# Routed experts of two batches: 46 tiles of their own against 40 shared tiles

## The chip, the core and the metric

The kernel runs on one NeuronCore of a Trainium2 chip. Five engines work side by side, each through its own queue in program order: PE (TensorE, matrix products and transposes), DVE (VectorE), ACT (ScalarE), POOL (GpSimd, here also the indirect DMAs) and SP (SyncE, here only DMA issues). A wait in a queue holds everything behind it. The metric is device microseconds of one execution. Before the change three runs gave 2401.68 us as median (2397.92 to 2402.32).

## What is computed

Two batches of 2048 tokens, 256 channels. First a bidirectional Mamba layer whose result is added to x with a gate; then a layer norm with scale and shift per batch, and a mixture of experts:

```
scores = softmax(xt @ gate_w.T);  top_vals, idx = top_k(scores, 2)
xs = xt[:, None, :] * weights[:, :, None]
y += sum_k( (silu(xs @ w1[e].T + b1[e]) @ w2[e].T + b2[e]) * (xs @ w3[e].T + b3[e]) )   # k with idx == e
z  = silu(xt @ sw1.T) * (xt @ sw2.T) @ sw3.T
out = x + gb * (y + z)
```

There are 8 experts, and each token goes to 2 of them. `gb` is a gate for each channel and batch.

## The kernel before, in words

The program has a long Mamba stage and then the expert stage (lines 928 to 1358), which is all that the change touches but for a few small DMAs. The expert stage has three parts.

**Units with fronts beside them** (lines 1278 to 1326). A batch has 4 chunks of 512 tokens. The shared expert of a chunk is 4 `hidden` units (line 1124: 16 matmuls in the trace, two PSUM banks, then silu on ACT and a product on DVE, line 1137) and 2 `result` units (line 1140: 16 matmuls, then an addition on DVE, line 1149). The list of units `interleaved` (line 1289) holds 37 places, k = 0 to 36, for the four chunks of the first batch and the first two of the second. What DVE and ACT do for a unit is put into their queues only after the next unit's matmuls (`unit`, line 1267). The table `beside` (line 1298) is an order written out by hand: it says which step of which chunk's `front` (line 988) is put in ahead of unit k. The steps are LOAD (two DMAs), OPEN (gate and add the Mamba result, then statistics, DVE), NORM (4 activations, ACT), MODULATE (scale and shift, DVE), TURN (8 transposes on PE, 2 copies on ACT), CHOOSE (router logits on PE, maximum and difference on DVE, exp on ACT) and RANK (two best experts, 14 small DVE operations). Seven PSUM banks, taken in turn (`bank`, line 935), serve units, TURN, CHOOSE and routing alike: an operation on PE waits until the bank used seven takes earlier has been read.

**Routing.** `route` (line 1057) works in two steps. The first counts on DVE; the second takes three small matmuls (lines 1073 to 1075) and then some 15 DVE operations, which give each token its two row numbers (`slots`) and each tile its expert (`owners`). `scatter` (line 1101) then writes 32 blocks of 128 weighted rows to DRAM (`xs`): a copy on ACT and an indirect DMA on POOL each. For the first batch that is routed at k = 15 and 16 and scattered two blocks a unit from k = 17.

**Tiles** (`expert_tiles`, line 1195). An expert's tokens are padded to tiles of 256 rows. Each batch has 23 tiles (`NTS`, the worst case), 46 in all. `load_tile` (line 1155) brings, three tiles ahead, three weight matrices of 256 KB, the biases and the tile's rows `xg`, all on SP's queue into four buffers. A tile on PE is four transposes of the rows (`qgT`), three products (`qh`, `q3`, `q2`) and four transposes back (`qyT`). ACT makes silu and the second factor with the gate folded in (line 1214, whose bias comes from a small DVE product, line 1206); DVE multiplies (line 1222) and copies `gT` (line 1186); ACT stores the result to `ys`. The second batch's last front steps, its routing and its scatter (4 blocks a tile) lie beside the first 16 tiles (`beside_tile`, `sides`, line 1330). After tile 25 the first batch is gathered chunk by chunk, every fifth tile, by 8 indirect DMAs (`gather`, line 1228); three tiles after a gather `combine` adds both parts to the sum (two DVE additions of 128x1024, line 1250), and SP stores it.

After the last tile the second batch is gathered, beside the shared units of its last two chunks; then come its combinations and stores (lines 1347 to 1358).

```
i = nc.gpsimd.indirect_dma_start(out=xs_d[b][:, :], in_=v, in_offset=None, ...)
tc.declare_no_dep(i, group=f"scatter{b}", reason="each writes rows of its own")
```

Every access is ordered after earlier ones to the same memory unless a line like this one excludes it; a scatter names the whole of `xs` as what it writes.

Of the kernel before, what the change touches and what calls it, by code (L numbers as in the profile page):

```python
# [35 lines left out]
NTS = (2 * T + E * (TS - 1)) // TS  # L36
# [4 lines left out]
def kernel(  # L41
# [26 lines left out]

    xs_d = [dram.tile([NTS * TS, C], F32, tag=f"xs{b}", name=f"xs{b}") for b in range(NB)]
    ys_d = [dram.tile([NTS * TS, C], F32, tag=f"ys{b}", name=f"ys{b}") for b in range(NB)]  # L70
# [63 lines left out]
    with tc.tile_pool(name="mw", bufs=1) as mw, tc.tile_pool(name="mw2", bufs=2) as mw2, \  # L134
# [690 lines left out]
        def early_small():  # L825
            early["wg"] = keep.tile([P, KC, E], F32, tag="wg", name="wg")
            nc.sync.dma_start(out=early["wg"], in_=gate.rearrange("(k p) e -> p k e", p=P))
            for b in range(NB):
                early["gbT", b] = keep.tile([P, KC], F32, tag=f"gbT{b}", name=f"gbT{b}")
                nc.sync.dma_start(out=early["gbT", b],  # L830
                                  in_=mod_d[b][0, 3 * C:4 * C].rearrange("(k p) -> p k", p=P))
# [19 lines left out]
        for s in range(NST + 4 + SPC):  # L851
# [42 lines left out]
            if i < NCH + 1:  # L894
                visit(i, k)
                if s == 8:
                    silu_gate(0)
                if k == 8 and 2 <= i < 2 + NB:
                    nc.sync.dma_start(out=xs_d[i - 2].rearrange("(p n) (m f) -> p (n m) f", p=P, f=P),
                                      in_=bc(ident, NTS * TS // P * 2))  # L900
# [14 lines left out]
        for _ in range(2):  # L915
            open_front(1)

# [10 lines left out]
    with tc.tile_pool(name="fw", bufs=1) as fw, tc.tile_pool(name="f1", bufs=1) as f1, \  # L928
# [27 lines left out]
        wg, gbTs = early["wg"], [early["gbT", b] for b in range(NB)]  # L956
# [19 lines left out]
        tiles = fw.tile([1, NTS, E], F32, tag="tiles", name="tiles")  # L976
        iotas = []
        for v, pattern in ((filled, [[0, E], [TS, NK]]), (tiles, [[1, NTS], [0, E]])):
            n = v.shape[1] * v.shape[2]
            w = f1.tile([v.shape[0], n], I32, tag=f"iota{n}", name=f"iota{n}")  # L980
            nc.gpsimd.iota(w, pattern=pattern, base=0, channel_multiplier=0)
            iotas.append((v, w))
# [72 lines left out]
        slots, owners = {}, {}  # L1055

        def route(b):
# [19 lines left out]
            nt = f1.tile([P, E], F32, tag="nt", name=f"nt{b}")  # L1077
            end = f1.tile([P, E], F32, tag="end", name=f"end{b}")
            nc.vector.tensor_tensor(more, pt.unsqueeze(2).to_broadcast([P, E, NK]), filled, ALU.is_gt)
            nc.vector.tensor_reduce(nt, more, AX.X, ALU.add)  # L1080
            nc.vector.tensor_tensor_scan(end, ones[:, 0:E], nt, 0.0, ALU.mult, ALU.add)
            nc.vector.tensor_tensor(nt, end, nt, ALU.subtract)
            nc.vector.tensor_scalar(nt, nt, float(TS), None, ALU.mult)
            nc.vector.tensor_tensor(past, ps.rearrange("p (e j) -> p e j", e=E),
                                    nt.unsqueeze(2).to_broadcast([P, E, NJ]), ALU.add)
            posf = f1.tile([P, 2, NJ], F32, tag="posf", name=f"posf{b}")
            for n in range(2):
# [4 lines left out]
            after = f1.tile([1, NTS, E], F32, tag="after", name=f"after{b}")  # L1092
            own = f1.tile([1, NTS], F32, tag="own", name=f"own{b}")
            nc.vector.tensor_tensor(after, tiles, end[0:1, :].unsqueeze(1).to_broadcast([1, NTS, E]),
                                    ALU.is_ge)
            nc.vector.tensor_reduce(own, after, AX.X, ALU.add)
            nc.vector.tensor_scalar(own, own, float(E - 1), None, ALU.min)
            owners[b] = fw.tile([1, NTS], I32, tag=f"own{b}", name=f"owner{b}")
            nc.vector.tensor_copy(owners[b], own)

        def scatter(b):
            sc = picks[b][1]
            for j in range(NJ):
                for n in range(2):
# [6 lines left out]
                        out=xs_d[b][:, :], in_=v, in_offset=None,  # L1111
                        out_offset=bass.IndirectOffsetOnAxis(ap=slots[b][:, n, j:j + 1], axis=0))
                    i = getattr(i, "ins", i)

                    tc.declare_no_dep(i, group=f"scatter{b}", reason="each writes rows of its own")
                    tc.add_to_no_dep_group(f"scatter{b}", i)
# [38 lines left out]
        def load_tile(b, i):  # L1155

            e = nc.sync.value_load(owners[b][0:1, i:i + 1], min_val=0, max_val=E - 1)
            ws = f4.tile([P, 3, KC, H], F32, tag="we", bufs=4, name=f"we{b}_{i}")
            xg = f4.tile([P, 2, C], F32, tag="xg", bufs=4, name=f"xg{b}_{i}")
            for n, src in enumerate((w1, w3, w2)):  # L1160
                nc.sync.dma_start(out=ws[:, n, :, :], in_=src[bass.ds(e, 1), :, :]
                                  .rearrange("o (k p) h -> p (o k) h", p=P))
            bs = f4.tile([P, 3, KH], F32, tag="bs", bufs=4, name=f"bs{b}_{i}")
            nc.sync.dma_start(out=bs, in_=b123[:, :, bass.ds(e, 1), :].rearrange("p n o k -> p n (o k)"))
            nc.sync.dma_start(out=xg, in_=tiled(xs_d[b][i * TS:(i + 1) * TS, :]))
            loaded[b, i] = ws, bs, xg
# [16 lines left out]
        def turned_in(b, i):  # L1183
            ps = turn_tile(loaded[b, i][2], f"qgT{b}_{i}")
            gT = f2.tile([P, KC, TS], F32, tag="gT", name=f"gT{b}_{i}")
            nc.vector.tensor_copy(gT, ps)  # L1186
            return gT

        def turned_out(b, i, x3):
            ps = turn_tile(x3, f"qyT{b}_{i}")  # L1190
            yo = f2.tile([P, 2, C], F32, tag="yo", name=f"yo{b}_{i}")
            nc.scalar.copy(yo, ps)
            nc.scalar.dma_start(out=tiled(ys_d[b][i * TS:(i + 1) * TS, :]), in_=yo)

        def expert_tiles(seq, sides):


            for k in range(3):
                load_tile(*seq[k])
            gT, x3 = turned_in(*seq[0]), None  # L1200
            for k, (b, i) in enumerate(seq):
                if k + 3 < len(seq):
                    load_tile(*seq[k + 3])
                ws, bs, _ = loaded.pop((b, i))
                b3 = f2.tile([P, KH], F32, tag="b3", name=f"b3{b}_{i}")
                nc.vector.tensor_tensor(b3, bs[:, 2, :], gbTs[b], ALU.mult)
                hT = f2.tile([P, KH, TS], F32, tag="hT", name=f"hT{b}_{i}")
                y3 = f2.tile([P, KC, TS], F32, tag="x3", name=f"x3{b}_{i}")
                ps = lin(ws, 0, gT, f"qh{b}_{i}")
                for m in range(KH):  # L1210
                    nc.scalar.activation(hT[:, m, :], ps[:, m, :], AF.Silu, bias=bs[:, 0, m:m + 1])
                ps = lin(ws, 1, gT, f"q3{b}_{i}")
                for m in range(KC):
                    nc.scalar.activation(y3[:, m, :], ps[:, m, :], AF.Identity,
                                         scale=gbTs[b][:, m:m + 1], bias=b3[:, m:m + 1])
                if k + 1 < len(seq):
                    gT = turned_in(*seq[k + 1])
                if x3 is not None:
                    turned_out(*seq[k - 1], x3)
                ps = lin(ws, 2, hT, f"q2{b}_{i}")  # L1220
# [4 lines left out]
                sides(k)  # L1225
            turned_out(*seq[-1], x3)

        def gather(b, q):
# [4 lines left out]
            for n in range(2):  # L1233
# [5 lines left out]
                for j in range(JC):  # L1239
                    nc.gpsimd.indirect_dma_start(  # L1240
                        out=v[:, j, :], out_offset=None, in_=ys_d[b][:, :],
# [5 lines left out]
        def combine(b, q, two):  # L1247
            x1 = x1s[b, q]
            for v in two:
                nc.vector.tensor_tensor(x1, x1, v, ALU.add)  # L1250
# [38 lines left out]
        def interleaved(keys):  # L1289

            units, due = [], []
            for k in keys:
# [5 lines left out]
        beside = {1: ((0, 0, CHOOSE), (0, 1, TURN)), 2: ((0, 2, OPEN),),  # L1298
                  4: ((0, 2, NORM), (1, 0, LOAD), (0, 0, RANK)),
                  5: ((0, 1, CHOOSE), (0, 2, MODULATE)), 6: ((1, 1, LOAD), (0, 3, OPEN)), 7: ((0, 2, TURN),),  # L1300
                  8: ((0, 3, NORM), (0, 1, RANK)), 9: ((0, 2, CHOOSE), (0, 3, MODULATE)), 11: ((0, 3, TURN),),
                  12: ((0, 2, RANK),), 13: ((0, 3, CHOOSE),), 14: ((0, 3, RANK),), 17: ((1, 0, OPEN),),
                  18: ((1, 2, LOAD),), 19: ((1, 0, NORM),), 20: ((1, 0, MODULATE), (1, 3, LOAD)),
                  21: ((1, 0, TURN), (1, 1, OPEN)), 22: ((1, 0, CHOOSE),), 23: ((1, 1, NORM),),
                  24: ((1, 1, MODULATE), (1, 0, RANK)), 26: ((1, 1, TURN),), 27: ((1, 1, CHOOSE),),
                  29: ((1, 1, RANK),), 30: ((1, 2, OPEN),), 32: ((1, 2, NORM),), 33: ((1, 3, OPEN),),
                  35: ((1, 3, NORM),)}
        beside_tile = {0: ((1, 2, MODULATE),), 1: ((1, 2, TURN), (1, 3, MODULATE)), 2: ((1, 2, CHOOSE),),
                       3: ((1, 2, RANK), (1, 3, TURN)), 4: ((1, 3, CHOOSE),), 5: ((1, 3, RANK),)}
        scatters, routes = [scatter(0), scatter(1)], [route(0), route(1)]  # L1310
        for k, f in enumerate(interleaved([(0, 0), (0, 1), (0, 2), (0, 3), (1, 0), (1, 1)])):
# [5 lines left out]
            if k in (15, 16):  # L1317
                follow(routes[0])
            unit(f)
            if k > 16:  # L1320
# [9 lines left out]
        def sides(k):  # L1330
            for p in beside_tile.get(k, ()):
                part(*p)
            if k in (6, 7):
                follow(routes[1])
            if k > 7:
                for _ in range(4):
                    follow(scatters[1])
            for q in range(NTC):
                if k == NTS + 2 + 5 * q:
                    twos[q] = gather(0, q)  # L1340
                if k == NTS + 5 + 5 * q:
# [3 lines left out]
        expert_tiles([(b, i) for b in range(NB) for i in range(NTS)], sides)  # L1345
# [69 lines left out]
```

## Time and profile before

The profiled execution took 2401.81 us; the profiler's span is 2400.0 us, so 1.8 us lie around it. Its own time is 0.13 us over the median of the three runs.

| what | value |
|---|---|
| PE busy | 1970.6 us, 82% |
| DVE busy | 2021.3 us, 84% |
| ACT busy | 1619.2 us, 67% |
| POOL busy | 1859.5 us, 77% |
| units with fronts | 1912 to 2059 us |
| tiles | 2059 to 2345 us |
| last shared units, gathers, stores | 2345 to 2400 us |

The shares are means over stages with different limits; the three last rows are read from the timeline. A line of the timeline gives start and duration in us, engine, source line, what is written from what, a count, and in brackets how long the engine sat idle before it and what ended that. A line of a window table gives for each engine busy us (and instructions), then the clock granted to PE (1.00 is full), the busy share of the DMA engines and GB/s.

### The profile page before, as it was taken

The numbers are of one execution on the slowest core, as the hardware profiler recorded it, in microseconds if no ns is written. First come the engines' busy times: TensorE is split into PE (matmuls) and PEld (weight loads), VectorE is DVE, ScalarE is ACT, GpSimd is POOL, SyncE is SP. The second block draws the span as 40 slices with busy tenths as digits, with TensorE's granted clock in tenths as the row PEclk, the third lists the DMA queues.
The fourth block names the chain that finished last, engine by engine and source line by source line (L and its number), as shares of the span: only waits on it lengthen the run. The fifth ranks groups of instructions, "written<-read, shape, count | busy, mean of one in ns | idle before, by whom it ended". The sixth has DMA issues, their size and how long they took to land. (4 is left out here: it accounts for less than half of the span.)

```text
span 2400.0 us, 30317 instructions
## 1 busy us (share of the span) xinstructions
PE 1970.6 (82%) x9512; PEld 1361.7 (57%) x9512; DVE 2021.3 (84%) x2691; ACT 1619.2 (67%) x3375; POOL 1859.5 (77%) x979
## 2 busy tenths in 40 slices
PE   5466878787978888787979788887976699999997
PEld 2133645555646555554656555554555566888884
DVE  5499999989999999999999999999999977542333
ACT  5557787868778787878787777878775334454331
POOL 0367898989999999999999999999999615041305
PEclk9677888898999889888989899998887899999999
DMA  4344447574544544445444444444456231587873
GB/s 161 110 161 155 150 158 226 182 235 165 170 159 158 177 157 169 161 157 176 153 165 163 163 151 167 157 160 159 132 172 224 90 112 73 174 262 239 264 238 114
DMA packets 239974, 403.08 MB, mean 168 GB/s; under 512 B 38818, under 2 KB 171938, under 8 KB 239812
## 3 DMA queue, kind: packets, MB, share of 16 engines
q1 hardware_dynamic: 220724, 370.72, 47.4%
q0 software_dynamic: 6144, 16.79, 2.0%
q10 hardware_dynamic: 12944, 13.64, 1.6%
q8 instruction: 75, 1.23, 0.2%
q14 instruction: 87, 0.71, 0.1%
HBM read 346.54 MB, written 54.53 MB: 167 GB/s over the span
## 5 line engine op out<-in xcount | busy, mean ns | idle before, releaser
L452 POOL TENSOR_TENSOR db<-du,B 128x1024 f32<-128x1024 f32 x452 | 1064.2, 2380 | 14.9 <-DMA B<-bcs 14.9
L496 POOL TENSOR_TENSOR db<-h,C 128x1024 f32<-128x1024 f32 x252 | 599.7, 2381 | 65.7 <-issue 53.9
L471 ACT ACTIVATE da<-dt,w_a 128x512 f32<-128x512 f32 x904 | 594.7, 688 | 79.2 <-DVE dt L336 46.2
L518 PE MATMUL y<-ident,db 128*128 128x128 f32 x4096 | 568.5, 287 | 39.1 <-POOL db L496 36.7
L518 PEld LDWEIGHTS y<-ident,db 128*128 128x128 f32 x4096 | 505.3, 150 | 160.6 <-issue 101.9
L485 DVE TENSOR_TENSOR_SCAN da<-da,hl,db 128x512 f32<-128x512 f32 x460 | 562.9, 1269 | 4.9 <-POOL db L452 3.7
L485 DVE TENSOR_TENSOR_SCAN h<-da,hl,db 128x512 f32<-128x512 f32 x444 | 540.1, 1263 | 15.5 <-ACT da L471 15.5
L491 DVE TENSOR_TENSOR db<-da,C 128x512 f32<-128x512 f32 x460 | 292.2, 676 | 19.8 <-DMA C<-bcs 12.5
L272 PE MATMUL psc<-xp,w_conv 128*128 128x512 f32 x512 | 235.2, 603 | 10.2 <-ACT xp L261 6.4
L255 PE MATMUL psx<-xT,w_in 128*128 128x512 f32 x256 | 155.8, 728 | 102.7 <-ACT hl L506 88.8
L390 PE MATMUL psz<-w_in,xT 128*128 128x512 f32 x256 | 151.1, 723 | 57.0 <-ACT bT L353 32.7
L1110 POOL DMA_INDIRECT xs<-xs,slot x64 | 63.6, 993 | 166.7 <-ACT xs L1106 100.6
L1240 POOL DMA_INDIRECT two<-ys,slot x64 | 63.5, 992 | 159.6 <-DMA ys<-yo 64.3
L342 POOL TENSOR_TENSOR du<-dt,xc 128x512 f32<-128x512 f32 x64 | 81.9, 1281 | 98.5 <-DVE dt L336 98.4
L272 PEld LDWEIGHTS psc<-xp,w_conv 128*128 128x128 f32 x512 | 93.9, 193 | 107.7 <-issue 96.0
L289 PE MATMUL psd<-xc,w_x 128*48 128x512 f32 x128 | 97.4, 932 | 67.7 <-ACT hl L506 47.6
L255 PEld LDWEIGHTS psx<-xT,w_in 128*128 128x128 f32 x256 | 49.8, 223 | 157.2 <-ACT hl L506 110.8
L418 PE MATMUL pso<-w_out,yg 128*128 128x256 f32 x512 | 118.4, 385 | 21.3 <-ACT e L312 20.0
L1186 DVE COPY gT<-qgT 128x512 f32<-128x512 f32 x46 | 31.8, 690 | 108.9 <-PE qgT L939 108.9
L506 ACT COPY hl<-da 128x1 f32<-128x1 f32 x460 | 61.5, 157 | 85.4 <-DVE db L491 82.8
L418 PEld LDWEIGHTS pso<-w_out,yg 128*128 128x128 f32 x512 | 95.6, 192 | 36.5 <-ACT e L312 22.9
L390 PEld LDWEIGHTS psz<-w_in,xT 128*128 128x128 f32 x256 | 53.1, 229 | 109.3 <-issue 42.0
(218 smaller groups left out, 3199.3 us busy)
## 6 DMA issues: line engine op xcount, KB each, us to landing
C<-bcs SPq DMA_DIRECT2D x256, 512.0 KB, 4.4
B<-bcs SPq DMA_DIRECT2D x226, 512.0 KB, 4.3
we<-in_w_dram SPq DMA_DIRECT2D x138, 256.0 KB, 3.7
acc<-acc SPq DMA_DIRECT2D x32, 512.0 KB, 5.5
xs<-ident SPq DMA_DIRECT2D x2, 5888.0 KB, 23.6
xg<-xs SPq DMA_DIRECT2D x46, 256.0 KB, 3.9
ys<-yo ACTq DMA_DIRECT2D x46, 256.0 KB, 3.0
xn<-xn SPq DMA_DIRECT2D x16, 512.0 KB, 5.9
```

The source lines that it names most:

```text
L255: nc.tensor.matmul(ps, w["in"][:, k, d * P:(d + 1) * P], v["xT"][:, k, :], start=(k == 0), stop=(k == KC - 1))
L272: nc.tensor.matmul(ps, w["conv"][:, d, k, :], v["xp"][:, d, k:k + TC], start=(k == 0), stop=(k == 3))
L289: nc.tensor.matmul(ps[:RK + 2 * NS, :], w["x"][:, d, :], v["xc"][:, d, :], start=(d == 0), stop=(d == ND - 1))
L342: nc.gpsimd.tensor_tensor(v["du"][:, d, :], v["dt"][:, d, :], v["xc"][:, d, :], ALU.mult)
L390: nc.tensor.matmul(ps, v["xT"][:, k, j * P:(j + 1) * P], w["in"][:, k, DI:2 * DI], start=(k == 0), stop=(k == KC - 1))
L418: nc.tensor.matmul(ps[:, n, :], v["yg"][:, d, n * P:(n + 1) * P], wo[:, d, :], start=(d == 0), stop=(d == ND - 1))
L452: nc.gpsimd.tensor_tensor(db, bc(ready[i]["du"][:, d, :], NG), live["B", s // 2], ALU.mult)
L471: nc.scalar.activation(da[n], ready[i]["dt"][:, d, :], AF.Exp, scale=w["a"][:, d, m:m + 1])
L485: nc.vector.tensor_tensor_scan(h[n], da[n], x[n], hl[:, d, m:m + 1], ALU.mult, ALU.add)
L491: nc.vector.tensor_tensor(live["db", s][:, n, :], h, live["C", s // 2][:, n, :], ALU.mult)
L496: nc.gpsimd.tensor_tensor(live["db", s], live.pop(("h", s)), live["C", s // 2], ALU.mult)
L518: nc.tensor.matmul(ys["y"][j // 2][:, j % 2, d % 2 * P:(d % 2 + 1) * P], src[:, j * P:(j + 1) * P], ident, is_transpose=True, start=(first ...
```

## The change

All tiles come from one list of 40 (`NT`). A batch-0 expert's whole tiles come first, then one tile for each of the 8 experts that holds its remaining tokens of the first batch and as many of the second as fit, then the second batch's further tiles. At least 9 tiles (`NF`) hold first-batch tokens only; the first batch lies within the first 24 (`N0`). `xs` and `ys` become one tensor each. Because a tile can hold both batches, the gate leaves the tile and goes to `combine`. All fronts and both routings are put among the units, with a new table `beside`; the second scatter runs beside tiles 0 to 7, and the first batch's gathers come every third tile.

```diff
-NTS = (2 * T + E * (TS - 1)) // TS
+NT = 2 * NB * T // TS + E
+NF = -((E * (TS - 1) - 2 * T) // TS)
+N0 = 2 * T // TS + E
+NQ = 3 * E + 1
...
-        tiles = fw.tile([1, NTS, E], F32, tag="tiles", name="tiles")
+        tiles = fw.tile([1, NT, NQ], F32, tag="tiles", name="tiles")
...
+            wide = [P, E, NJ]
+            at = ps.rearrange("p (e j) -> p e j", e=E)
+            nc.vector.tensor_tensor(both, at, whole.unsqueeze(2).to_broadcast(wide), ALU.is_ge)
+            nc.vector.tensor_tensor(both, both, jump.unsqueeze(2).to_broadcast(wide), ALU.mult)
+            nc.vector.tensor_tensor(past, at, start.unsqueeze(2).to_broadcast(wide), ALU.add)
+            nc.vector.tensor_tensor(past, past, both, ALU.add)
...
+            nt, nq = (NF, E) if b == 0 else (NT, NQ)
...
+            nc.vector.tensor_tensor(after, tiles[:, 0:nt, 0:nq],
+                                    bound[:, 0:nq].unsqueeze(1).to_broadcast([1, nt, nq]), ALU.is_ge)
+            if b:
+                nc.vector.tensor_tensor(after, after, growth.unsqueeze(1).to_broadcast([1, nt, nq]), ALU.mult)
             nc.vector.tensor_reduce(own, after, AX.X, ALU.add)
...
+        def apart(i, own, others, reason):
+
+            i = getattr(i, "ins", i)
+            for group in others:
+                tc.declare_no_dep(i, group=group, reason=reason)
+            tc.add_to_no_dep_group(own, i)
...
-                        out=xs_d[b][:, :], in_=v, in_offset=None,
+                        out=xs_d[:, :], in_=v, in_offset=None,
...
+                    apart(i, f"scatter{b}", (f"scatter{b}", f"load{b}"), "each writes rows of its own")
...
+            d = nc.sync.dma_start(out=xg, in_=tiled(xs_d[i * TS:(i + 1) * TS, :]))
+            if i < NF:
+                apart(d, "load1", ("scatter1",), "full of the first batch's tokens")
...
-                b3 = f2.tile([P, KH], F32, tag="b3", name=f"b3{b}_{i}")
-                nc.vector.tensor_tensor(b3, bs[:, 2, :], gbTs[b], ALU.mult)
...
-                    nc.scalar.activation(y3[:, m, :], ps[:, m, :], AF.Identity,
-                                         scale=gbTs[b][:, m:m + 1], bias=b3[:, m:m + 1])
+                    nc.scalar.activation(y3[:, m, :], ps[:, m, :], AF.Identity, bias=bs[:, 2, m:m + 1])
...
-            for v in two:
-                nc.vector.tensor_tensor(x1, x1, v, ALU.add)
+            nc.vector.tensor_tensor(v, v, w, ALU.add)
+            nc.vector.tensor_tensor(v, v, bc(mods[b][:, 3, :], JC), ALU.mult)
+            nc.vector.tensor_tensor(x1, x1, v, ALU.add)
...
+        beside = {0: ((1, 0, LOAD), (1, 1, LOAD)), 1: ((0, 0, CHOOSE), (0, 1, TURN)), 2: ((0, 2, OPEN),),
+                  3: ((0, 1, CHOOSE),), 4: ((0, 2, NORM), (0, 0, RANK)),
+                  5: ((0, 2, MODULATE), (1, 2, LOAD)), 6: ((0, 3, OPEN),), 7: ((0, 2, TURN), (0, 1, RANK)),
+                  8: ((0, 3, NORM), (0, 2, CHOOSE)), 9: ((0, 3, MODULATE), (1, 3, LOAD)), 10: ((1, 0, OPEN),),
+                  11: ((0, 3, TURN), (0, 2, RANK)), 12: ((1, 0, NORM), (0, 3, CHOOSE)),
+                  13: ((1, 0, MODULATE), (0, 3, RANK)), 15: ((1, 0, TURN),), 16: ((1, 1, OPEN),),
+                  17: ((1, 0, CHOOSE),), 18: ((1, 1, NORM), (1, 0, RANK)), 19: ((1, 1, MODULATE),),
+                  20: ((1, 2, OPEN),), 21: ((1, 1, TURN),), 22: ((1, 2, NORM), (1, 1, CHOOSE)),
+                  23: ((1, 2, MODULATE), (1, 1, RANK)), 24: ((1, 3, OPEN),), 25: ((1, 2, TURN),),
+                  26: ((1, 3, NORM), (1, 2, CHOOSE)), 27: ((1, 3, MODULATE), (1, 2, RANK)),
+                  29: ((1, 3, TURN),), 30: ((1, 3, CHOOSE),), 32: ((1, 3, RANK),)}
...
-            if k in (15, 16):
-                follow(routes[0])
+            if k in (14, 15, 33, 34):
+                follow(routes[k // 33])
             unit(f)
-            if k > 16:
+            if k > 15:
...
+        def sides(i):
+            for _ in range(4):
+                follow(scatters[1])
             for q in range(NTC):
-                if k == NTS + 2 + 5 * q:
+                if i == N0 + 1 + 3 * q:
                     twos[q] = gather(0, q)
-                if k == NTS + 5 + 5 * q:
+                if i == N0 + 4 + 3 * q:
                     combine(0, q, twos.pop(q))
                     store(0, q)
```

Smaller edits: the two loads of the gate as a column go, the fill of `xs` with finite numbers ahead of time shrinks from twice 5888 KB to twice 5120 KB, and `route` of the first batch gets some ten more small DVE operations for the bounds of the three groups of tiles.

## Prediction

> **What bounds the kernel now.** I read the page's engine shares first, then its slices, the chain that ended last, the windows of the expert stage, and last the timeline. The Mamba stage keeps DVE at 9 tenths until 1880 us; the change reaches it only by two DMAs of 1 KB less and a smaller fill, so I leave it out. From 1922 us the chain runs on PE.
>
> ```profile
> PE q L1172 7%; PE pg L1131 4%; PE qh L1172 3%; PE pz L1146 2%; PE qyT L939 1%; PE qgT L939 1%; PE fpsl L1022 0%; PE fpsT L939 0%; POOL two L1240 0%; DMA two<-ys,slot 0%; DVE st L96 0%; DVE x L92 0%; DVE fac L91 0%; DVE hs L1137 0%; DVE sm L97 0%
> ```
>
> The windows (busy us of PE, PEld, DVE, ACT, POOL; clock; DMA share; GB/s) say how near the next engine is:
>
> ```profile
> 1920.00:1926.00 6.00, 5.47 (x13) 3.31 (x14) 1.45 (x4) 3.44 (x6) 3.82 (x7) 0.53 1.07 376
> ...
> 1940.00:1960.00 20.00, 20.00 (x82) 13.32 (x81) 18.83 (x51) 9.62 (x15) 0.00 (x0) 1.00 0.16 54
> 1960.00:1980.00 20.00, 20.00 (x81) 13.25 (x80) 11.84 (x40) 5.57 (x8) 0.00 (x0) 1.00 0.00 0
> ...
> 2040.00:2059.00 19.00, 17.85 (x66) 12.14 (x65) 12.81 (x44) 6.02 (x12) 4.65 (x10) 1.00 0.48 150
> sum 147.00, PE 142.91 PEld 89.88 DVE 105.09 ACT 62.36 POOL 44.54; mean PE 15.88 PEld 9.99 DVE 11.68 ACT 6.93 POOL 4.95
> ```
>
> So among the units PE is full while DVE works 105 of 147 us. The tiles repeat like this, with PE never idle:
>
> ```profile
> 2326.64 1.89 PE L1172 MATMUL qh<-gT,we 128*128 128x256 f32 x8
> 2328.37 1.89 PE L1172 MATMUL q<-gT,we 128*128 128x256 f32 x8
> 2330.10 0.60 PE L939 MATMUL qgT<-ident,xg 128*128 128x128 f32 x4
> 2330.53 0.60 PE L939 MATMUL qyT<-ident,x 128*128 128x128 f32 x4
> 2330.97 1.89 PE L1172 MATMUL q<-hT,we 128*128 128x256 f32 x8
> 2332.70 1.89 PE L1172 MATMUL qh<-gT,we 128*128 128x256 f32 x8
> ```
>
> One tile is 2332.70 - 2326.64 = 6.06 us. At the end it is gathers, then DVE:
>
> ```profile
> 2388.05 6.01 DVE L1250 TENSOR_TENSOR x<-x,two 128x1024 f32<-128x1024 f32 x5
> 2390.39 0.96 POOL L1240 DMA_INDIRECT two<-ys,slot  x1 [0.30 <-issue]
> 2394.30 1.23 DVE L1250 TENSOR_TENSOR x<-x,two 128x1024 f32<-128x1024 f32 x1 [0.25 <-DMA two<-ys,slot]
> ```
>
> **Six tiles less.** 46 become 40 by the constants. PE is the bound in all of them, so 6 x 6.06 = **-36.3**. The gate's product (L1206, 0.15 us) hid behind PE; it gives nothing.
>
> **Moved fronts.** PE's share of what moves (two TURN of 0.87, two CHOOSE of 1.71, the three routing products 0.6: 5.8 us) leaves the tiles and comes back among the units: 0. On DVE it is different, for in the tiles DVE had room and among the units it has little. Part by part from the timeline: OPEN 7.25 us (1988.08 to 1995.33), MODULATE 2.40, CHOOSE 0.33, RANK 4.05 (1934.10 to 1938.13), hs 0.61, pz addition 0.60, the second step of routing 4.1 (1983.39 to 1987.48). Added: 2 x (2.40 + 0.33 + 4.05) = 13.6; ten more small operations and three of 128x128 at 0.29 in the first routing, 2.6; the first step of the second routing, 1.3; the counter's cast some 0.7. The second routing's second step: on one partition 184 elements take 0.33 us and 1024 elements elsewhere 1.22, so each of the three operations on 40 x 25 = 1000 takes about 1.2 instead of 0.33; with 0.8 for small ones and 0.9 for the wide ones I get 8.9. Together 27 us on 105 in a stretch of 147: 132, of which some must be waits.
>
> Where do they fall? I set the parts of each order out on the queues of PE, DVE and ACT, each starting when its engine is free, its operands are there and the bank seven takes back has been read. For the order before this ends at 2058.1 (trace 2059.0), with DVE waiting 3.5 us for psr (trace 3.2) and PE 1.7 us for hs (trace 1.15). For the new order PE waits 1.2 us at k = 9, 2.1 at 12, 3.4 for the first psr at 15 (RANK of chunk 3 and the first step stand ahead of it on DVE), 2.5 at 16 (banks behind the 6.7 us of routing), 0.9 at 21, 4.1 at 22 (a bank behind OPEN of (1,2)), 0.7 at 26, and **8.5 at 35**: the second routing stands at k = 34, so its 8.9 us on DVE run ahead of the product hs of the last hidden unit, which the next result unit needs after 3 of its 8 groups. Sum 23.3 against 2.2 before: **+21.1**. If DVE's parts run 3% faster or slower the walk gives 18.9 or 23.1; 18.4 is its least.
>
> **Clock.** After a wait of PE of 2.67 us the granted clock was near half for some 5 us (the first window above):
>
> ```profile
> 1920.53 1.94 PE L939 MATMUL fpsT<-ident,fac_early 128*128 128x128 f32 x8 [2.67 <-DVE s L1028]
> 1922.26 15.57 PE L1131 MATMUL pg<-fxT,s 128*128 128x512 f32 x32
> 1937.66 1.85 PE L1022 MATMUL fpsl<-wg,fxT 128*128 128x8 f32 x16
> ```
>
> From 1920.53 to 1937.66 is 17.1 us for work that later takes 0.87 + 4 x 3.43 = 14.6: 2.5 us lost. After 1.15 us at 2051.6 nothing was lost. The waits of 3.4, 4.1 and 8.5 us should each cost up to 2.5. While DVE sets the pace most of the first two is hidden; the last is paid in full. I take **+3.5**, between 0 and 7.5. The Trainium skill ("TensorE: Matmul & The Clock Gate", Part 1) says that the clock halves after an idle window of about 3.4 us and comes back after 3.4 busy ones; it speaks against this change. By it a wait would cost 1.7 us, so an estimate of 3.4 to 5.1 for two or three waits; the row here shows more, and already at 2.67.
>
> **Second scatter against the loads.** Tiles below 9 are exempted, but with 4 blocks a tile only 24 of 32 are queued before `load_tile(9)`. So load 9 waits for block 24, blocks 25 to 28 (they name all of `xs`) wait for load 9, load 10 for them, the last four for load 10, load 11 for those. Behind the waiting load on SP stand the next weights; behind the waiting scatter on POOL only scatters.
>
> ```profile
> 2133.18 0.96 POOL L1110 DMA_INDIRECT xs<-xs,slot  x1 [1.14 <-ACT xs L1106]
> ...
> 2136.98 0.96 POOL L1110 DMA_INDIRECT xs<-xs,slot  x1 [0.19 <-issue]
> ```
>
> These are a tile's four (its first product at 2126.80): the fourth is issued 10.2 us after the tile's start T. There a block lands after 4.1 us (3.1 to 5.0), a load of `xg` after 3.9. Block 24 is there at T5 + 14.3 = T7 + 2.2, load 9 at T7 + 6.1, the next four at T7 + 14.1, load 10 at T7 + 18.0 = T9 + 5.9. PE turns tile 10 at T9 + 3.46 (2330.10 - 2326.64): 2.4 late. The next round takes 12 us against 6.06 for a tile: 6.0 more. With 3.1 for a landing it is 3.5 in all, with these 8.4: **+6**, and **+2** for the clock after the longer wait (0 to 2.5). The trace of before has no such wait; if the order is not enforced it is 0.
>
> **Combining.** Three additions or products instead of two, 1.20 us each. In the tiles DVE has room (0.5 us idle before the next gT, which PE needs 1.3 us later). At the end nine operations follow 2388.05 instead of six with a wait: 2388.05 + 9 x 1.20 = 2398.9 against 2395.5: **+3.3**.
>
> **Gathers every third tile.** The DMA share is 0.72 in tiles without gather (2181 to 2205 us) and 0.85 as mean over two rounds of gather, store and late loads (2242 to 2302); the 0.13 x 30.3 = 4 us of a round in 18.2 us make 0.94. A store holds SP until its combine is done: the load behind the first (xg at 2249.36, 5.0 us late) lands about 2254 and is needed at 2257; 1.2 us more leave some 2. I take 0, at worst some 2 us at each of four.
>
> **Sum.** -36.3 + 21.1 + 3.5 + 6 + 2 + 3.3 = -0.4 us, on the profiled 2401.81: **2401.4**. That execution lies 0.1 us over the median of the runs.
>
> **Rivals.** *The cover holds* (0.28): the clock isn't lowered when DVE sets the pace, and scatter and load pass each other. Then -36.3 + 18.4 + 3.3 = -14.6: 2387; with half of that 2394. For it: the DVE queue is the one part that I checked against the trace. *The clock* (0.30, the slower side): each of the waits of 2.5, 3.4, 4.1, 8.5 and 6 us is paid with 2.5, 12.5 instead of 5.5: +7, so 2408; with the long scatter round (+2.4) and slower DVE parts (+2) 2413. It decides from 5.2 us over my sum, that is when four of the five are paid nearly in full and one other cost is at its upper end. Against it: where DVE is late anyway, a slow PE loses nothing. *DMA as bound* in tiles 25 to 38 is in the same 0.30: four late loads, 8 us, 2409. *PE still the bound everywhere* would be -33, 2369; the window with DVE at 18.8 of 20 excludes it for me (below 0.02, within the faster case).
>
> **How the numbers follow.** What a measurement here can tell from no change is about 0.2%, 4.8 us. My forecast's own case (gain and waits cancel to within that) has 0.42, faster 0.28, slower 0.30. The range goes from 2387 (the cover holds) to 2413 (clock, long round, slower DVE).
>
> **What would show it.** Tiles of 6.06 us, 40 times; DVE at 9 tenths from 1925 to 2055 and PE at 8 to 9 there; one PE wait of 8 to 9 us for hs before the last two result units; qgT of tiles 10 and 11 waiting for xg; 9 operations of 1.2 us at the end. I am wrong if PE is full among the units, if the tiles show no wait at 10 and 11, or if tiles 25 to 39 wait for loads.

## The result, and the profile after

The changed kernel takes 2384.04 us (median of 4 runs, 2380.47 to 2386.42) against 2401.27 us for the kernel before beside it: a ratio of 0.9929, 95% interval 0.9912 to 0.9947. It is faster by 17 us, and the predicted 2401.4 us and its range from 2387 both lie above it. Its profiled execution took 2383.38 us, the span is 2381.4 us.

The first thing to do with such a miss is to cut both timelines at the same events. The start is the first `pg` of the units, then the first `qgT` of the tiles, then the last `qyT`, then the end of the span:

| stage, us | before | after | difference | predicted |
|---|---|---|---|---|
| Mamba, until the first `pg` | 1912.5 | 1907.8 | -4.7 | 0, left out |
| units | 146.6 | 170.7 | +24.2 | +30.4 (21.1 waits, 3.5 clock, 5.8 of PE's work moved in) |
| tiles | 286.2 | 244.9 | -41.2 | -34.1 (-36.3 - 5.8 + 8 for scatter and load) |
| end | 54.8 | 57.9 | +3.1 | +3.3 |
| sum | 2400.0 | 2381.4 | -18.6 | -0.4 |

Three of the four rows are off, all in the same direction. This is the chain that ended last on the page of after; DVE has 5% of it, where before it had 1%:

```profile
PE 13%; DVE 5%; ACT 1%; issue 1%; DMA 0%; POOL 0%; POOLq 0%; DVEq 0%; ACTq 0%
PE q L1224 6%; PE qh L1224 3%; PE pg L1181 2%; PE pz L1196 1%; PE qgT L942 1%; PE qyT L942 1%; DVE hs L1187 0%; DVE st L99 0%; ACT L1186 0%; DVE x L95 0%; DVE fac L94 0%; DVE xh L116 0%; POOL two L1289 0%; DVE sm L100 0%; ACT hs L1186 0%
```

The windows of after over the units (columns as before):

```profile
1940.00:1960.00 20.00, 20.00 (x84) 13.07 (x83) 18.80 (x53) 8.31 (x14) 0.00 (x0) 1.00 0.17 54
1960.00:1980.00 20.00, 15.99 (x71) 11.26 (x71) 16.39 (x57) 7.34 (x12) 0.00 (x0) 0.97 0.00 0
1980.00:2000.00 20.00, 20.00 (x66) 12.12 (x67) 15.98 (x65) 6.49 (x12) 3.42 (x6) 0.86 0.18 54
2000.00:2020.00 20.00, 20.00 (x75) 11.70 (x74) 14.93 (x43) 12.35 (x25) 10.01 (x19) 1.00 0.18 66
...
2060.00:2078.53 18.53, 10.69 (x42) 8.30 (x41) 9.22 (x26) 0.30 (x1) 0.00 (x0) 0.82 0.56 167
```

PE is full again from 1980 to 2020 (at first at a lower clock), where the prediction had it waiting for banks at k = 16, 21 and 22. Its idle time sits mainly in two windows: 4 us around 1976 to 1980, and 7.8 us near the end. PE's timeline of after names both:

```profile
1979.75 0.79 PE L1084 MATMUL psr<-both,before 128*128 128x128 f32 x2 [3.61 <-DVE both L1075]
1980.54 0.80 PE L1085 MATMUL psr<-past,ones 128*128 128x128 f32 x2
1981.13 0.43 PE L1086 MATMUL psr<-lastn,ones 128*128 128x8 f32 x2
1981.41 9.27 PE L1181 MATMUL pg<-fxT,s 128*128 128x512 f32 x16
...
2061.81 1.54 PE L1196 MATMUL pz<-s,hs 128*128 128x256 f32 x6
2071.19 7.50 PE L1196 MATMUL pz<-s,hs 128*128 128x256 f32 x26 [7.84 <-DVE hs L1187]
2078.53 0.60 PE L942 MATMUL qgT<-ident,xg 128*128 128x128 f32 x4
```

The second wait follows six matrix products of `pz`, as predicted for the result unit after the second routing. The other waits over 0.3 us are 2.68 (as before), 0.40, 0.89 and 0.62. In the tiles, 35 of the 39 steps from one tile to the next take 6.05 or 6.06 us, as before; the two lines at 2302 and 2308 are an example. There is one new wait in 40 tiles, at 2144.83 (0.94 us at the first tile and 0.64 us at the last stand in the kernel before too, with 0.99 and 0.65):

```profile
2144.83 0.66 PE L942 MATMUL qgT<-ident,xg 128*128 128x128 f32 x4 [0.91 <-DMA xg<-xs]
...
2302.34 0.60 PE L942 MATMUL qgT<-ident,xg 128*128 128x128 f32 x4
...
2308.39 0.60 PE L942 MATMUL qgT<-ident,xg 128*128 128x128 f32 x4
```

POOL's timeline shows that scatter and load do alternate there; each scatter here waited for a load of `xg`:

```profile
2126.05 0.96 POOL L1163 DMA_INDIRECT xs<-xs,slot  x1 [4.82 <-DMA xg<-xs]
...
2135.78 0.96 POOL L1163 DMA_INDIRECT xs<-xs,slot  x1 [4.87 <-DMA xg<-xs]
```

### The profile page after: what moved, and what is told of

It reads as the page before. It is cut to its first block, busy times and chain, and to the rows that moved or that the text cites. A ratio compares the mean times of both kernels' runs of the same rounds, so it can differ in the third digit from the quotient of the medians.

```text
span 2381.4 us, 29700 instructions
## 1 busy us (share of the span) xinstructions
PE 1943.5 (82%) x9320; PEld 1333.1 (56%) x9320; DVE 2025.1 (85%) x2658; ACT 1600.9 (67%) x3345; POOL 1858.6 (78%) x983
## 5 line engine op out<-in xcount | busy, mean ns | idle before, releaser
L488 DVE TENSOR_TENSOR_SCAN h<-da,hl,db 128x512 f32<-128x512 f32 x444 | 540.5, 1265 | 17.7 <-ACT da L474 17.7
L1181 PE MATMUL pg<-fxT,s 128*128 128x512 f32 x256 | 117.3, 611 | 1.8 <-DVE hs L1187 0.9
```

The lines of the kernel that those rows point to most:

```text
L488: nc.vector.tensor_tensor_scan(h[n], da[n], x[n], hl[:, d, m:m + 1], ALU.mult, ALU.add)
L1181: nc.tensor.matmul(ps, s12[:, n, k, m * P:(m + 1) * P], xTs[b, q][:, k, :], start=(k == 0), stop=(k == KC - 1))
```

## The experiments

The first eight kernels ran on another chip than the runs above. On it the kernel before takes 2454 to 2458 us, but was not profiled. The changed kernel takes 2423.6 us there, and its profiles put the loss into the tiles and the end, where engines get some instructions late (last section). The Mamba stage and the units show none of this: the units of `after_again` take 170.72 us there too. So stages are compared, and total times only by their ratio to the kernel before on the same chip, where the changed kernel has 0.9886 (0.9859 to 0.9912). By their totals only `hs_first` and `scatter_six` differ from it clearly; the intervals of the others overlap with it, and what they show is read from the stages.

### The same again

No edit.

> The changed kernel, nothing altered, as the base for the three runs beside it. Its profile should show the units' stage at 170.7 us again (the order of the instructions, not chance, sets it) and PE's waits of 3.6 us for psr and 7.8 us for hs at their places; a stage that differs by more than 1 us would say that differences of single microseconds between kernels can't be read from one profile.

Measured: 2423.59 us; units 170.72 us, waits of 3.60 and 7.83 us at their places. In the six profiles with this order of the units the stage repeats to 0.03 us, so differences there can be read from one profile. The start of the units doesn't repeat so well: in seven profiles with the changed kernel's fill it lies between 1905.3 and 1908.8 us.

### The fill of `xs`

`fill_long` makes the two fills as long as before (5888 KB each, the second overlapping the first); `fill_split` makes twenty of 512 KB.

```diff
-                    n = NT * TS // NB
+                    n = 23 * TS
...
```
```diff
-                if k == 8 and 2 <= i < 2 + NB:
-                    n = NT * TS // NB
+                if k % 8 == 4 and 2 <= i < 7:
+                    n, u = 2 * TS, (i - 2) * 4 + k // 8
...
```

> The changed kernel, with the two early fills of xs as long as before (5888 KB each, overlapping by 1536 KB). Theory A (the Mamba stage got 4.7 us shorter because SP's queue stands behind a shorter fill: the B load behind it took 14.1 instead of 16.7 us): 4 to 5 us slower than the changed kernel, units beginning near 1912 again. Theory B (the 4.7 us are chance or come from elsewhere): within 1.5 us of the changed kernel, units beginning near 1908.

> The changed kernel, with the fill in 20 pieces of 512 KB, one every eighth step. Theory A: DVE and POOL no longer wait for B and C behind a fill (some 7 us left in the changed kernel between 380 and 620 us), so 5 to 7 us faster than the changed kernel, units beginning near 1901. Theory B: within 1.5 us of it.

Measured: the units begin at 1914.02 with the long fill, at 1903.08 with the split one (2433.45 and 2425.06 us, ratios 0.9902, 0.9887 to 0.9917, and 0.9858, 0.9839 to 0.9877). The groups of the Mamba stage carry it; after the bar stand busy time and mean of one, after the second bar the idle time ahead of the group. First the page of before, then after, then the long and the split fill:

```profile
L452 POOL TENSOR_TENSOR db<-du,B 128x1024 f32<-128x1024 f32 x452 | 1064.2, 2380 | 14.9 <-DMA B<-bcs 14.9
```
```profile
L455 POOL TENSOR_TENSOR db<-du,B 128x1024 f32<-128x1024 f32 x452 | 1061.6, 2369 | 9.0 <-DMA B<-bcs 9.0
```
```profile
L455 POOL TENSOR_TENSOR db<-du,B 128x1024 f32<-128x1024 f32 x452 | 1061.4, 2367 | 15.5 <-DMA B<-bcs 15.5
```
```profile
L455 POOL TENSOR_TENSOR db<-du,B 128x1024 f32<-128x1024 f32 x452 | 1061.6, 2368 | 2.1 <-DMA B<-bcs 2.1
```

The length of the fill alone sets POOL's wait for `B`; DVE's wait for `C` goes the same way, with 12.5, 5.5, 13.2 and 0 us. On SP, the next load of `B` behind the fill occupies the queue for 16.65 us before, 14.14 us after. Over all profiles of the study, the units begin at 1910.9 to 1914.0 us with long fills (four, mean 1912.8), 1905.3 to 1908.8 with the shorter ones (seven, mean 1906.9), and 1896.8 to 1905.2 with split ones (three, mean 1901.7). Kernels that are alike in this stage spread, the split ones by 8.3 us, so one pair can't price the fill; but long and shorter fills don't overlap. By the means the smaller fill is worth about 6 us, which fits the 4.7 of the pair above.

### PSUM's banks taken strictly in turn

```diff
-            tc.tile_pool(name="ps_f", bufs=7, space=PSUM) as ps_f, \
+            tc.tile_pool(name="ps_f", bufs=1, space=PSUM) as ps_f, \
...
-            return ps_f.tile([P, TC], F32, tag="mm", name=name)
+            turn = taken[0] = (taken[0] + 1) % 7
+            return ps_f.tile([P, TC], F32, tag=f"mm{turn}", name=name)
```

> The changed kernel, with the seven PSUM banks of the expert stage taken strictly in turn, as my prediction assumed. Theory A (the walk through the queues was right but for the banks, which in truth go to whichever was given back first in program order): PE waits for banks behind k = 9, 12, 16, 21 and 22, in sum 8 to 11 us, stage and total 4 to 9 us longer than in the changed kernel. Theory B (banks are not what made the walk too long): within 1.5 us of the changed kernel.

Measured: 2435.04 us (0.9901, 0.9887 to 0.9915); units 177.07 us, 6.35 more. The waits that the prediction had at k = 9, 12, 16, 21 and 22 are now there. PE's timeline of this kernel (all its waits over 0.5 us between 1940 and 2070 but the two of psr):

```profile
1953.27 7.13 PE L1183 MATMUL pg<-fxT,s 128*128 128x512 f32 x16 [0.88 <-DVE x_early L1201]
...
1965.90 1.92 PE L1035 MATMUL fpsl<-wg,fxT 128*128 128x8 f32 x16 [1.19 <-DVE mx L1044]
...
1988.57 1.98 PE L1183 MATMUL pg<-fxT,s 128*128 128x512 f32 x4 [1.16 <-DVE hs L1189]
...
2006.73 1.06 PE L944 MATMUL fpsT<-ident,xh 128*128 128x128 f32 x8 [0.62 <-PE pg L1183]
...
2015.19 3.56 PE L1035 MATMUL fpsl<-wg,fxT 128*128 128x8 f32 x16 [3.96 <-DVE x L1201]
```

4.2 of the 6.35 us are waits (17.6 against 13.4, added up below). The rest is slower products, above all behind the wait of 3.96 us: `fpsl` takes 3.56 us there and 1.85 in the changed kernel.

The last wait against the changed kernel: DVE's order is the same in both, and its addition of `pz` to `x` comes late behind the same OPEN part (2014.36 here, 2013.77 there). This is PE's and DVE's timeline of after at the same place:

```profile
2010.47 1.85 PE L1033 MATMUL fpsl<-wg,fxT 128*128 128x8 f32 x16
```
```profile
2013.77 0.68 DVE L1199 TENSOR_TENSOR x<-x,pz 128x512 f32<-128x512 f32 x1
```

`fpsl` starts 3.3 us before the addition that I had made it wait for. It took a bank that had been given back earlier, not the oldest one.

### The product of the last hidden unit ahead of the second routing's second step

```diff
-            if k in (14, 15, 33, 34):
+            if k in (14, 15, 33):
                 follow(routes[k // 33])
             unit(f)
+            if k == 34:
+                follow(routes[1])
```

> The changed kernel, with the last hidden unit's silu and product queued ahead of the second routing's second step instead of behind it. Theory A (PE's 7.8 us wait at the end of the units, and 1.9 us of lowered clock after it, come from the place of the routing on DVE): the wait goes; gT of the first tile stands behind the routing instead, a wait of 3 to 4 us; 6 to 7.5 us faster than the changed kernel. Theory B (the work on DVE has to be waited for in any case): within 2 us of the changed kernel.

Measured: 2419.11 us (0.9839, 0.9824 to 0.9854); units 161.08 us, 9.64 less. PE's timeline at the end of the units:

```profile
2051.93 7.03 PE L1181 MATMUL pg<-fxT,s 128*128 128x512 f32 x16
...
2059.38 7.15 PE L1196 MATMUL pz<-s,hs 128*128 128x256 f32 x32
2066.37 0.60 PE L942 MATMUL qgT<-ident,xg 128*128 128x128 f32 x4
2070.07 1.99 PE L1224 MATMUL qh<-gT,we 128*128 128x256 f32 x8 [3.10 <-DVE gT L1238]
```

The wait is gone, and so is what followed it: `pz` runs at full clock. 9.64 is 7.84 of waiting and 1.8 of clock. DVE's routing work now delays gT, which PE waits for 3.10 us instead of 0.95 at the first tile. So 2.15 come back, and the edit is worth about 7.5.

### The first routing later

```diff
-            if k in (14, 15, 33, 34):
+            if k in (15, 17, 33, 34):
...
-            if k > 15:
+            if k > 17:
```

> The first routing goes to k = 15 and 17 instead of 14 and 15, so that its first step has a whole unit less work of DVE ahead of it. Theory A (the wait of 3.6 us for psr and the low clock behind it, about 3 us, are a real loss of PE): the units' stage falls from 170.7 to 164 to 167 us. Theory B (DVE sets the pace from k = 9 to k = 22, so that a wait of PE at one place only stands for one at the next): the wait goes and others of 1 to 3 us come at k = 16 to 22, the stage within 1.5 us of 170.7.

Measured: 2427.80 us (0.9896, 0.9865 to 0.9926); units 169.29 us, 1.43 less. The products of the routing wait for nothing, but soon PE waits for the part that DVE couldn't do meanwhile:

```profile
1982.61 0.47 PE L1084 MATMUL psr<-both,before 128*128 128x128 f32 x2
...
1987.73 7.17 PE L1196 MATMUL pz<-s,hs 128*128 128x256 f32 x32 [0.77 <-DVE hs L1187]
...
2001.35 1.94 PE L942 MATMUL fpsT<-ident,xh 128*128 128x128 f32 x8 [3.01 <-DVE xh L117]
```

3.6 us of waiting went and 3.78 came. In this kernel DVE works from 1969.9 to 2014 without a wait over 0.3 us, so DVE sets the pace there, and the place of PE's wait says little of what a cure is worth. The second theory holds by the number, but narrowly, and 1.43 understates the edit. Up to the wait for hs near the end the stage is 2.85 us shorter; behind that wait the same products take 8.75 us, where the changed kernel needs 7.34:

```profile
2066.41 8.91 PE L1196 MATMUL pz<-s,hs 128*128 128x256 f32 x26 [7.83 <-DVE hs L1187]
2075.16 0.60 PE L942 MATMUL qgT<-ident,xg 128*128 128x128 f32 x4
```

### Six blocks of the second scatter a tile

```diff
-            for _ in range(4):
+            for _ in range(6):
                 follow(scatters[1])
```

> Six blocks of the second scatter per tile instead of four, so that all 32 are queued before the first load that may read them. Theory A (the alternation of scatter and load exists, but landings of 2.4 and 2.8 to 3.4 us make it short): PE's one wait for a late xg, 0.91 us at tile 11, goes, and with it the POOL waits of 4.8 us for xg; 0.9 us less in the tiles. Theory B (the alternation also costs PE's clock, or holds SP's weights back): 3 to 6 us less. Theory C: load 9 now waits for all 32 blocks instead of 24, and a new wait of 2 us or more stands at tile 9.

Measured: 2441.26 us (0.9953, 0.9937 to 0.9969), 20.2 us more in the tiles than `after_again`. The wait of PE for `xg` at tile 11 (1.15 us in `after_again`) and POOL's waits for it are gone, as the first theory says, and no wait stands at tile 9, against the third. But others came: 5.13 us at 2099.7 ("issue") and 9.37 at 2133, with late instructions around them; the 8.82 us at 2278 have their like in `after_again`, 9.98 at 2257. On a chip like that of the result the same edit (in `best_six`, below) costs 2.4 us in the tiles: two waits of 1.43 and 1.52 us come, and the 0.82 for `xg` goes. Its timeline shows how: ACT scales the blocks and has to wait until a scatter has read the buffer; `hT` stands behind it, and PE behind `hT`. First ACT, then PE:

```profile
2095.40 0.51 ACT L1159 ACTIVATE xs<-xh,sc 128x256 f32<-128x256 f32 x1 [2.86 <-DMA xs<-xs,slot]
2095.81 0.82 ACT L1261 ACTIVATE hT<-qh,bs 128x256 f32<-128x256 f32 x2
```
```profile
2096.32 1.99 PE L1224 MATMUL q<-hT,we 128*128 128x256 f32 x8 [1.52 <-ACT hT L1261]
```

None of the three theories had this wait. That the longer ones on the other chip begin in the same way is only argued; why instructions come late there stays open.

### The gate alone, in the kernel before

```diff
-                    nc.scalar.activation(y3[:, m, :], ps[:, m, :], AF.Identity,
-                                         scale=gbTs[b][:, m:m + 1], bias=b3[:, m:m + 1])
+                    nc.scalar.activation(y3[:, m, :], ps[:, m, :], AF.Identity, bias=bs[:, 2, m:m + 1])
...
-            for v in two:
-                nc.vector.tensor_tensor(x1, x1, v, ALU.add)
+            nc.vector.tensor_tensor(v, v, w, ALU.add)
+            nc.vector.tensor_tensor(v, v, bc(mods[b][:, 3, :], JC), ALU.mult)
+            nc.vector.tensor_tensor(x1, x1, v, ALU.add)
```

> One part of the change alone, in the kernel before: the gate goes from the activation of the third product to the combining sums (three vector operations a chunk instead of two). Theory A (at the end of the kernel the vector engine's row of operations is what ends last, in the tiles it has room): tiles unchanged, the end 3.1 to 3.4 us longer, nothing else; 0.13% of the time, hardly to be seen in it. Theory B (the last gathers set the end, and the two more operations per chunk hide behind them): less than 1 us.

> The kernel before, nothing altered, to see its stages on the chip of these runs. If the late instructions of PE, DVE and ACT in the tiles and at the end belong to the chip, they are here too: Mamba stage and units as on the first chip (units 146.6 us), tiles 10 to 25 us over 286.2, the end 15 to 22 us over 54.8. If they come only with the changed kernel, tiles and end are within 2 us of the first chip's.

These two, and the two kernels with the parts together, ran on a chip where the kernel before takes 2402.02 us, as in the result. Measured: the kernel before again 2402.48 us (ratio 1.0002, 0.9993 to 1.0011), with units 146.56, tiles 286.17, end 54.60 us. That run can't say whether the other chip's late instructions hit the kernel before in the same stages, which is what it was for; only its 2454 to 2458 us there speak for it. The gate alone: 2406.26 us, 1.0024 (1.0015 to 1.0033); units 146.54, tiles 286.35, end 58.39 us. So the end is 3.6 to 3.8 us longer and nothing else moves. DVE's timeline, the last three of nine in a row without a gap:

```profile
2393.98 1.22 DVE L1246 TENSOR_TENSOR two<-two,two 128x1024 f32<-128x1024 f32 x1
2395.23 1.22 DVE L1247 TENSOR_TENSOR two<-two,fmod 128x1024 f32<-128x1024 f32 x1
2396.49 1.23 DVE L1248 TENSOR_TENSOR x<-x,two 128x1024 f32<-128x1024 f32 x1
```

### DVE's work at the end earlier

The three operations of the second batch's chunk 1 and two of chunk 2 are issued during the last shared units; the last chunk is gated source by source, the second in halves.

```diff
+            if k == 10:
+                combine(1, 1, twos.pop(1))
+                store(1, 1)
+                v, w = twos[2]
+                nc.vector.tensor_tensor(v, v, w, ALU.add)
+                nc.vector.tensor_tensor(v, v, bc(mods[1][:, 3, :], JC), ALU.mult)
...
-        for q in range(1, NTC):
-            combine(1, q, twos.pop(q))
-            store(1, q)
+        nc.vector.tensor_tensor(x1s[1, 2], x1s[1, 2], twos[2][0], ALU.add)
+        store(1, 2)
+        v, w = twos[3]
+        for a, js in ((v, slice(0, JC)), (w, slice(0, JC // 2)), (w, slice(JC // 2, JC))):
+            x1 = x1s[1, 3][:, js, :]
+            nc.vector.tensor_tensor(a[:, js, :], a[:, js, :], bc(mods[1][:, 3, :], js.stop - js.start), ALU.mult)
+            nc.vector.tensor_tensor(x1, x1, a[:, js, :], ALU.add)
+        store(1, 3)
```

> Of the nine vector operations at the end, the three of chunk 1 and the first two of chunk 2 of the second batch are issued earlier, and the last chunk is taken without the joint sum, its second half in two halves. If the end of the kernel is set by DVE's row of nine operations of 1.22 us (theory A), the end gets 2.4 to 3.6 us shorter, until the last gathers set it; if it is set by the gathers on POOL and their landing (theory B), it gets less than 1 us shorter.

Measured: 2422.48 us (0.9881, 0.9854 to 0.9908), the same as `after_again` within the interval, since the tiles took 3.3 us longer with late instructions. The end is 74.35 against 79.03 us, 4.7 less; but on that chip the seven kernels without the edit spread from 77.4 to 79.4 us, so the 54.14 against 57.93 us of the next kernel, 3.8 less, are the better number. DVE's row set the end, by a little more than I expected. In the next kernel it stops for the last gather, for 0.67 us:

```profile
2359.13 0.69 DVE L1413 TENSOR_TENSOR two<-two,fmod 128x512 f32<-128x512 f32 x1 [0.67 <-DMA two<-ys,slot]
```

### The parts together

The split fill, the order at k = 34, the later first routing and the earlier end, with four blocks a tile (`best_four`) or six (`best_six`).

> The changed kernel with the four edits that shortened their stages: the fill in twenty pieces, the first routing later, the product of the last hidden unit ahead of the second routing's second step, the end's vector work earlier; scatters stay at four a tile. If the parts add up: 3 to 5 us (fill) + 9.6 (order at the end of the units) + 1.4 (routing later) + 4 (end) = 18 to 20 us less than the changed kernel's 2423.6 on such a chip, a ratio of about 0.980 to the kernel before. If the vector engine sets the pace of the units, as the run with the routing later suggests, order and routing give less than 11 us together.

> The same with six scatters a tile. Theory A (the 17.7 us that six scatters a tile cost before come from instructions arriving late while the indirect transfers are dense): again 10 to 20 us slower than with four, with waits of PE, ACT and DVE for nothing that the profile shows at tiles 2 to 10. Theory B (that run was hit by chance): within 3 us of the run with four.

Measured: `best_four` 2366.43 us (0.9840, 0.9821 to 0.9859; the changed kernel had 0.9929), `best_six` 2368.62 us (0.9865, 0.9850 to 0.9880). In `best_four` the units begin at 1905.2, take 158.10 us (12.6 less than in the changed kernel, where order and routing alone gave 9.6 and 1.4), tiles 247.00 (the wait for gT among them), end 54.14. That is 17 us less in the span than the changed kernel, where I expected 18 to 20: the sum had left out the 2.15 us that come back in the tiles. Order and routing together give more than 11 us, against the last sentence of my expectation: with the wait for hs gone, the later routing also keeps the 1.4 us that it lost behind that wait when alone. With six blocks the whole is within 3 us of four, as the second theory says, but the tiles take 249.43 us, 2.4 more. (Its units begin 8.3 us earlier with the same instructions up to there, and that is the spread of the Mamba stage.)

## Why the prediction was wrong

It is 18.2 us over the profiled change of -18.6: 4.7 in the Mamba stage, 6.2 in the units, 7.1 in the tiles, 0.2 at the end. That the faster rival (2387) comes near the result is luck: its premises don't hold, for the clock was lowered, and scatter and load do wait for each other.

**Right.** Six tiles at 6.06: nearly every tile takes that, and -41.2 is -36.3, less 5.8 of PE's work that moved, plus 0.9. The wait for hs (8.5 predicted, 7.84 measured) at its place, and the second routing step on DVE, where 8.9 us were predicted and 8.5 measured, with 1.18, 1.19 and 1.18 us for the three operations on one partition. The psr wait is at its place too, but its size (3.4, 3.61) is partly luck: with the banks as the prediction had them, PE waits there for 1.95 us only. The end: +3.3 predicted, 3.1 in the pair, 3.6 to 3.8 for the gate alone. The gathers every third tile cost nothing: no wait in tiles 25 to 39.

**"The bank seven takes back has been read".** This is the step that failed in the units, as far as the runs show. I assumed that banks go round strictly. The rotation alone, put in by hand, costs 6.35 us and brings five of the six bank waits back; the compiled program as it is gives a product a bank that came back earlier. I had compared the walk with the kernel before, where no product waits for a bank, so agreement there (2058.1 against 2059.0) proved nothing about this premise. Even with it the walk counted too much: its 23.3 us of waits are 17.6 with the strict rotation (0.88, 1.19, 1.95, 1.16, 0.62, 3.96 and 7.83), and 13.4 in the changed kernel. So the banks explain 4.2 of the 9.9 us; the other 5.7 are spread over all eight waits, none of them over 1.5, and why the walk made each a little too long stays open. Against 1.15 before, waits cost +12.2, not +21.1. With 5.8 of PE's work and 5.0 of clock (next) that is 23.0 of the 24.2; the rest, 1.2, is in waits and slow products too short to list.

**The clock** was mis-sized the other way. The row of after: the granted clock is 0.50 from 1979.5 to 1984.5, behind the wait of 3.61, and 0.50 from 2071 to 2074, behind that of 7.84.

```profile
1979.50:1984.50 5.00, 4.75 (x10) 2.87 (x11) 4.25 (x23) 0.00 (x0) 0.00 (x0) 0.50 0.01 3
...
2071.00:2074.00 3.00, 2.81 (x7) 2.27 (x8) 0.14 (x1) 0.00 (x0) 0.00 (x0) 0.50 0.07 25
2074.00:2077.00 3.00, 3.00 (x14) 2.62 (x13) 0.69 (x1) 0.00 (x0) 0.00 (x0) 0.91 0.00 0
```

Psr and 16 products of `pg` took 10.77 us (1979.75 to 1990.52) for 7.46 at full clock, and `pz` 7.34 for 5.68: 3.3 + 1.7 = 5.0, where I took 3.5. By the Trainium skill ("TensorE: Matmul & The Clock Gate", Part 1) a wait costs an estimated 1.7 us; the second wait agrees, the first exceeds it by 1.6. The agreement is chance: behind the same wait of 7.83 us 2.1 us were lost in `banks_in_turn` and 3.1 in `route_later`, behind 3.96 us 4.5 in `banks_in_turn`, and behind the 3.10 us for gT in `hs_first` none, with a granted clock of 1.00. No single price for a wait fits these runs. And `route_later` shows that of the first wait and the slow products behind it, 6.9 us together, at most 2.85 were a loss, since DVE sets the pace there: that part of the reasoning holds in the main.

**Scatter against loads: 8 predicted, 0.9 measured.** The mechanism is there: POOL waits 4.8 and 4.9 us for the load, and PE waits for `xg` at tile 11. The size was off because I took landings of 4.1 and 3.9 us from one tile. Here a load went out 2.4 to 2.5 us after the block that it waited for (2120.16 to 2122.63, 2129.85 to 2132.25). Over the whole kernel scatters land in 2.5 us at the median after the change (3.2 before), and the loads of `xg` issued at 2122.63 and 2132.25 let POOL go after 3.4 and 3.5 us. My first round holds two landings of each kind; with 2.5 and 3.5 us it gets 4.0 us shorter, and its 2.4 us late at tile 10 become none, as measured. The next round took 9.7 us (2126.05 to 2135.78) where I had 12. With no long wait the clock term fell too. That the queues are emptier there because the next weights are held behind the waiting load is only argued.

**"The change reaches it only by two DMAs of 1 KB less and a smaller fill, so I leave it out".** The smaller fill was seen, and not priced. POOL and DVE wait for the `B` and `C` that stand behind it on SP's queue, and POOL is busy nearly all of that stage. The page of before had it, in its costliest line: 14.9 us of idle time on POOL for `B`. 768 KB less on each of two fills took 6 us of it; the fill's length was a term of the sum, about 6 us for 13% of it.

## What to carry to other kernels

A transfer with no consumer nearby is still on the path of what is queued behind it: look for the idle time at its queue, not at its result, and split it. A walk over the queues is worth what its premises on buffers are worth: test it on a row where they bind, or price the sum with and without them. And a wait on an engine is a loss only if the engine that it waits for has room; where that one sets the pace, the wait moves.

## What the runs showed of the hardware

On the other chip, PE, ACT and DVE got some instructions late, in the tiles and in the last units, while indirect transfers of POOL were running. PE's timeline of `after_again` where the changed kernel's is without gaps:

```profile
2373.27 0.59 PE L1181 MATMUL pg<-fxT,s 128*128 128x512 f32 x1 [0.84 <-issue]
2376.76 1.01 PE L1181 MATMUL pg<-fxT,s 128*128 128x512 f32 x1 [2.91 <-issue]
2378.87 1.01 PE L1181 MATMUL pg<-fxT,s 128*128 128x512 f32 x1 [1.09 <-issue]
```

"issue" is time in which nothing that the profile shows was waited for; the profiles from that chip lack the landings of DMAs, so their releasers are less certain. Its tiles took 264.56 us instead of 244.94, its end 79.03 instead of 57.93. One explanation would be that the loading of the program competes with the gathers. The trace speaks against it: the packets of kind "instruction" after 2070 us are 24 in both profiles and take 17.7 us in all against 17.1, and none falls between 2346 and 2421 us, where PE's late products above lie. The cause stays open. Also new to me: one fill of 5 MB holds the loads behind it on the queue for 14 us, and twenty of 512 KB cost POOL 2.1 us in all where two of 5 MB cost 9.0.
